# Layers' turned rows in 128-byte pieces, other PSUM banks, other prices for the listing

## The chip, the cores and the metric

The kernel runs on one core of a Trainium2 chip. The time is device microseconds of the whole execution on that core. The engines are TensorE (PE; its weight loads are listed apart as PEld), VectorE (DVE), ScalarE (ACT), GpSimd (POOL) and SyncE (SP), which here only issues transfers. Before the change three runs gave a median of 1317.81 us (1317.18 to 1320.26).

## What is computed

128 graphs of 64 nodes with 256 features each run through four layers, each with a layer normalisation ahead of it and a residual sum behind it. All numbers are float32.

```python
h = relu(layernorm(x)); x = x + L0(h, adj)   # attention, 4 heads: softmax over edges, then elu
h = relu(layernorm(x)); x = x + L1(h, adj)   # attention, 1 head
h = relu(layernorm(x)); x = x + L2(h, adj)   # gated relations; entries of adj are 0 or 1, so only relation 1 counts
h = relu(layernorm(x)); x = x + L3(h, adj)   # 3 steps: a = A^T (h W_i), then a GRU cell on (a, h)
```

In an attention layer the weight of edge (i, j) is exp(leaky_relu(s_i + d_j)) over its sum, where s and d are products of the node's row with two vectors. Up to a factor that the sum takes out, this is the larger of two products, so the kernel makes exp((alpha - 1) s_i), exp(d_j) and exp(alpha d_j) and combines them with max. For adjacencies with entries over 1 a general path exists, which isn't entered here.

## The kernel before

**Tiling.** Two graphs of 64 nodes fill the 128 partitions, and four such pairs make a group (`G = 4`, 512 rows). There are 16 groups. Each goes through layers 0, 1 and 2 (`attention` at line 1383, twice, and `loop_relation` at 1473) and then three steps of the recurrence (`Recurrence.step` at 1059). The products of the recurrence are most of the kernel's: a step has 42 products of 128 x 128 by 256 columns, each of two passes. Two groups' recurrences alternate, and the layers of later groups lie between them.

**The order of the work is written by a planner.** All instructions are recorded first (`Plan.note` at 254, called by `Engine` at 539; so almost all of them have line 549 in the profile, and those of `beside` have 841). Then `Plan.emit` (503) lists them with modelled durations (`cost` at 583): it runs forward and backward `PASSES` times with a random seed `SEED`, takes the best, shifts jobs by the numbers in `MOVES`, and emits the result. So each engine has a fixed order, and waits in it. For a transfer, `cost` takes bytes over a rate that hangs on the tile's tag. Where the listing sees PE idle in the first 115 us, it emits filler products (`nc.spare`, line 1638, `sz<-warm`), one for each 220 ns of that idle time (line 530).

**PSUM.** There are eight banks. `Banks.room` (1231) gives `sy` two, `sz` three, and three to a shared tag `mt`, which serves `tp`, `tq`, `mm` and `mn`. The recurrence's sets of seven products (`Sevens` at 1066) take one `sy` and one `sz` bank each; there are four sets in a step, 192 in all.

**The turned rows of the layers.** The products of layers 0 to 2 need the normalised rows with features on partitions. For the first two groups PE transposes them (`layernorm_T`, 695). For the other 14 groups `layernorm_T_by_dma` (734) does so, 42 times: ScalarE writes the normalised rows `hn`, VectorE turns blocks of 32 x 32 into `tb`, one transfer takes `tb` to DRAM (`way`, 512 KB), four more bring it back to `land`, each into 32 partitions (1 KB pieces), and two ScalarE copies of 512 columns put it in its place in `hT`. `tb` and `land` share the buffers `hn`, so the trace has them as `hn`. The recurrence has its own round trips through `way`, to `hnat` and `hT`, which also serve the start of a recurrence.

**Edges and exponentials.** Each group's adjacency is loaded thrice: `at` as four transfers of 32 KB (two graphs of a pair on the free axis), `ag` with 128 nodes on the partitions, and `eg` turned. `edge_bounds` (1365) makes from `at` a bound for each edge, transposed by PE. For the 14 later groups, `attention` brings the s exponentials `fs` onto all partitions: PE transposes `fs`, VectorE copies it to `fT`, one transfer writes `row` to DRAM, and two read it back to `t`, the same to all 64 partitions of a half.

**Queues.** Almost all transfers go through SP's queue, in its fixed order.

Of the kernel before, what the change touches and what calls it, by code (L numbers as in the profile page):

```python
# [10 lines left out]
F32 = mybir.dt.float32  # L11
# [6 lines left out]
S = 32  # L18
# [9 lines left out]
NEG1 = -9000000000000000.0  # L28
ALPHA = 0.2
EPS = 1e-5  # L30
BIG, TINY = 3.0e38, 1.0e-24
BOUND = 6.25
NREL = 39
RC = 5
# [188 lines left out]
class Plan:  # L223
# [30 lines left out]
    def note(self, engine, call, cost, writes, reads, after=(), port=0.0, dma=False):  # L254
# [23 lines left out]
            b.ops.append(op)  # L278
        return op

    PASSES, SEED, SPREAD = 27, 39, 50.0
    MOVES = (
        10, 12, 18, 24, 27, 28, 58, 71, 83, 84, 89, 99, 118, 129, 136, 141, 144, 198, 214, 221, 266, 299, 322, 324,
        334, 341, 346, 390, 400, 412, 424, 434, 550, 559, 579, 611, 616, 682, 785, 808, 825, 869, 910, 1123, 1323,
        1710, 1729, 1754, 1784, 1908, 1924, 1933, 2133, 2158, 2174, 2755, 2883, 3921, 3988, 4026, 4270, 4596, 4876,
        4885, 5049, 5501, 5547, 5750, 5954, 6055, 6156, 6434, 6590, 7283, 7340, 7414, 7540, 7602, 7657, 7774, 7857,
        7930, 7942, 8201, 8457, 8683, 8685, 9083, 9436, 9811, 9967, 10320, 10820, 10999, 11484, 11701, 12627, 12696,
        12718, 12783, 12858, 12980, 13024, 13178, 13347, 13474, 14022, 14057, 14422, 14846, 16253, 16751, 16786,
        17194, 18227, 19571, 21611, 22526, 22951, 22990, 23107, 24055, 25299,
    )  # L290
    LEEWAY = {"PE": 100.0, "DVE": 100.0, "Activation": 100.0, "Pool": 100.0, "SP": 300.0, "-": 0.0}
    OVERLAP = {"DVE": 83.0, "Activation": 95.0, "Pool": 43.0}
# [210 lines left out]
    def emit(self):  # L503

        self.on = False
        self.link()
        best, self.random = None, Random(self.SEED)
        for _ in range(self.PASSES):
            ranks = [op.due for op in self.ops]
            end, order = self.forward()  # L510
            if best is None or end < best[0]:
                best = end, ranks, [op.start for op in self.ops]
            self.backward(end)
        end, ranks, starts = best
        jobs = list({id(op.job): op.job for op in self.ops}.values())
        for j in jobs:
            j.sum, j.count, j.shift = 0.0, 0, dict.fromkeys(self.RANKED, 0.0)
        for op, start in zip(self.ops, starts):
            op.job.sum, op.job.count = op.job.sum + start, op.job.count + 1
        for m in self.MOVES:  # L520
            self.move(m, end, jobs)
        for op, due in zip(self.ops, ranks):
            op.due = due + op.job.shift.get(op.engine, 0.0)
        end, order = self.forward()
        best = end, [(op, op.start, op.idle, op.places) for op in order]
        self.ends = best[0]
        for op, start, idle, places in best[1]:
            op.start = start
            if op.engine == "PE" and self.spare and start < 115.0 * 1e3:
                for _ in range(int((idle - 100.0) / 220.0)):  # L530
                    self.spare()
            for b, tag in places:
                b.pool.make(b, tag)
            op.call()
        self.ops = []
        return best[0]
# [46 lines left out]
def cost(engine, method, args, kwargs):  # L583
# [4 lines left out]
        return (m / 1.2 + 2.5) * (1 if method == "transpose" else 2)  # L588
    if engine == "sync" or method == "dma_start":
        to, of = args[:2]  # L590
        rate = {"way": 450.0, "fine": 220.0}.get(to.base.tag, 150.0) if isinstance(to, View) else 150.0
        if isinstance(of, View) and of.base.tag in ("way", "fine"):
            rate = 170.0 if of.base.tag == "way" else 125.0
        return n * to.shape[0] * 4 / rate
# [15 lines left out]
def kernel(  # L610
# [33 lines left out]
    xr = x.rearrange("b n d -> (b n) d").rearrange("(t q) d -> q t d", q=P)  # L644
    ar = adj.rearrange("b n m -> (b n) m").rearrange("(t q) m -> q t m", q=P)

    tr = adj.rearrange("(t r a) i j -> t a i r j", r=2, a=2)
    er = adj.rearrange("(t r a) j i -> t r j a i", r=2, a=2)
    outr = out.rearrange("b n d -> (b n) d").rearrange("(t q) d -> q t d", q=P)

# [7 lines left out]

    same = nc.kept(const, [P, P], F32, name="same")
    diag = nc.kept(const, [P, N], F32, name="diag")  # L660
    amax = nc.kept(const, [P, NG], F32, name="amax")
    flag = nc.kept(const, [1, 1], I32, name="flag")
    wc = nc.kept(const, [P, LAYERS, K, 3 * D], F32, name="wc")
    whh = nc.kept(const, [P, K, 3 * D], F32, name="whh")
# [69 lines left out]
    def layernorm_T_by_dma(work, dram, src, hT, natural=None):  # L734
# [50 lines left out]
        nc.vector.transpose(  # L785
            tb.rearrange("p j k n c -> p n k j c"), hn.rearrange("p n (k j b) -> p n k j b", k=K, b=S)
        )
        way = dram.tile([P, P // S, K * n * S], F32, name="way")
        nc.sync.dma_start(way, tb.rearrange("p j k n c -> p j (k n c)"))
        land = work.tile([P, P // S, K * n, S], F32, name="land")  # L790
        for j in range(P // S):
            nc.sync.dma_start(
                land[j * S : (j + 1) * S].rearrange("p i x c -> p i (x c)"),
                way[:, j].rearrange("(i b) x -> b i x", b=S),
            )
        for a in range(2):
            nc.scalar.copy(
                hT[:, a].rearrange("p k n (e c) -> p (k n) e c", c=S),
                land[:, 2 * a : 2 * a + 2].rearrange("p e x c -> p x e c"),
            )  # L800

    def transpose_blocks(psum, dst, src, rblocks, scale=1.0, turned=False):
# [416 lines left out]
    with ExitStack() as s1:  # L1219
# [4 lines left out]
        class Banks(Pool):  # L1224
# [4 lines left out]
            early = psum = spare = True  # L1229

            def room(self, tag, base):
                return {"mt": 3, "sy": 2, "sz": 3}.get(tag, 1)


            def tile(self, shape, dtype, name, **kwargs):
# [31 lines left out]
        class Layer:  # L1267

            place = {"em": "hn", "dg": "hn", "tb": "hn", "land": "hn"}

            shared = {"hn": 3, "o": 2, "st": 4, "mv": 4, "var": 4, "rstd": 4, "nm": 4, "rec": 4, "fT": 1}

            def __init__(self, layer, pool, bufs):
                self.layer, self.pool, self.bufs = layer, pool, bufs
# [16 lines left out]
        for i, a in enumerate((a_src, a_dst)):  # L1293
            nc.scalar.dma_start(AB[:, i, :], over_partitions(a, D))
        nc.scalar.dma_start(w0e[:, :, :D], rows(W0))
        AT, XG, AG, EG = [], [], [], []

        def load_group(g):
            nc.begin(("load", g))
            xg = work.tile([P, G, D], F32, name="xg", bufs=5)  # L1300
            n = 2 if g == 0 else G
            for p in range(0, G, n):
                nc.sync.dma_start(xg[:, p : p + n], xr[:, g * G + p : g * G + p + n, :])
            at = work.tile([P, G // 2, 2, N], I32, name="at", bufs=3)
            for a in range(2):
                for u in range(G // 2):
                    edges = tr[g * G // 2 + u, a]
                    nc.sync.dma_start(at[a * N : (a + 1) * N, u], edges)
            AT.append(at)
            XG.append(xg)  # L1310

        def load_edges(g):
            ag = work.tile([P, G, N], I32, name="ag", bufs=4)
            nc.sync.dma_start(ag, ar[:, g * G : (g + 1) * G, :])
            AG.append(ag)
            eg = work.tile([P, G, N], I32, name="eg", bufs=2)
            for r in range(2):
                for u in range(G // 2):
                    nc.sync.dma_start(eg[r * N : (r + 1) * N, 2 * u : 2 * u + 2], er[g * G // 2 + u, r])
            EG.append(eg)  # L1320
# [44 lines left out]
        def edge_bounds(g):  # L1365


            at = AT[g]
            top = work.tile([P, G // 2, 2], F32, name="top")
            nc.vector.tensor_reduce(top, at, AX.X, ALU.max)  # L1370
            nc.vector.tensor_reduce(amax[:, g : g + 1], top, AX.XY, ALU.max)
            nc.vector.tensor_scalar(top, top, 0.0, TINY, op0=ALU.is_le, op1=ALU.mult)
            m = work.tile([P, G // 2, 2, N], F32, name="m", bufs=1)
            nc.vector.tensor_scalar(m, at, 0.0, BIG, op0=ALU.is_gt, op1=ALU.mult)
            nc.vector.tensor_tensor(m, m, top[:, :, :, None].to_broadcast([P, G // 2, 2, N]), ALU.max)
            pt = psum.tile([P, T], F32, name="tp")
            for u in range(G // 2):
                nc.tensor.transpose(pt[:, u * P : (u + 1) * P], m[:, u].rearrange("p g j -> p (g j)"), ident)
# [4 lines left out]
        def attention(g, p0, n, layer, heads, we, pool):  # L1383
# [31 lines left out]
                    )  # L1415
            else:

                fs = pool.tile([P, n, heads], F32, name="fs")
                nc.scalar.activation(fs, es[:, :, :heads], AF.Exp, scale=ALPHA - 1.0)
                pt = psum.tile([P, T], F32, name="tp")  # L1420
                nc.tensor.transpose(pt[:nh, :P], fs.rearrange("p g h -> p (g h)"), ident)
                fT = pool.tile([nh, P], F32, name="fT")
                nc.vector.tensor_copy(fT, pt[:nh, :P])
                row = dram.tile([2, nh * N], F32, name=f"row{layer}")
                nc.sync.dma_start(row.rearrange("a (c i) -> c a i", i=N), fT.rearrange("c (a i) -> c a i", i=N))
                for half in range(2):
                    nc.sync.dma_start(
                        t[half * N : (half + 1) * N].rearrange("p c i -> p (c i)"),
                        row[half : half + 1, :].to_broadcast([N, nh * N]),
                    )  # L1430
            flat = lambda d, c: d.rearrange("p g h -> p (g h)")[:, c, None].to_broadcast([P, len(range(nh)[c]), N])
            m = 2 if heads > 1 else n
# [95 lines left out]
        def before(g):  # L1528
            ABD[g] = work.tile([P, G, N], F32, name="abd")
            by_dma = dram if g >= AHEAD else None  # L1530
            START[g] = before_recurrence(W[3], psum, XG[g], AG[g], ABD[g], by_dma, g in PLAIN)

        def recur(g):
            return Recurrence(
# [99 lines left out]
        if 115.0:  # L1634
            warm = const.tile([P, P], F32, name="warm")
            nc.nc.vector.memset(warm, 1.0)
            pause = psum.real.tile([P, P], F32, name="sz", tag="sz", bufs=3)
            nc.spare = lambda: psum.spare and nc.nc.tensor.matmul(pause, warm, warm, start=True, stop=True)  # L1638
        with tc.manual_schedule(engines={getattr(mybir.EngineType, e) for e in ENGINES.values()}):
            nc.emit()  # L1640
# [215 lines left out]
```

## Time and profile before

One profiled execution took 1316.05 us, of which the span that the profile shows is 1314.2. TensorE had its full clock through it.

| What | Value |
|---|---|
| Median of the runs | 1317.81 us |
| The profiled execution, its span | 1316.05 us, 1314.2 us |
| Busy TensorE in the first 88 us | 85.04 us |
| Busy TensorE in the last 64 us | 54.77 us |
| DMA share of 16 engines: first 33 us, 88 to 1186 | 79%, 37% |
| Packets on SP's queue, their bytes | 132,072, 142.54 MB |
| Packets under 512 bytes | 43,417 of 132,782 |

Three rows of the trace about the pieces that the change touches: the filler, the transposes of the exponentials (two shapes, for layers 0 and 1), and the copies of them on VectorE. Columns are line, engine, operation, output and inputs, shape, count, then busy time in us, mean ns of one, and the idle time ahead of them.

```profile
L1638 PE MATMUL sz<-warm 128*128 128x128 f32 x168 | 24.5, 294 | 1.1 <-DVE mhalf L549 1.1
...
L549 PE MATMUL tp<-ident,fs 128*16 128x128 f32 x14 | 3.8, 273 | 0.0
L549 PE MATMUL tp<-ident,fs 128*4 128x128 f32 x14 | 3.8, 273 | 0.0
```

Products overlap in PE's pipeline, so the mean time of one (294 ns) is longer than the spacing of two (0.11 us in the timeline). A filler product is two passes, so 168 passes are 84 products.

The list of transfers has, with bytes of one and the median us from issue to landing:

```profile
way<-hn SPq DMA_DIRECT2D x42, 512.0 KB, 3.0
hn<-way SPq DMA_DIRECT2D x168, 128.0 KB, 3.1
```

The first is `tb` on its way to DRAM, the second the way back to `land`.

### The profile page before, as it was taken

The numbers are of one execution on the slowest core, as the hardware profiler recorded it, in microseconds if no ns is written. First come the engines' busy times: TensorE is split into PE (matmuls) and PEld (weight loads), VectorE is DVE, ScalarE is ACT, GpSimd is POOL, SyncE is SP. The second block draws the span as 40 slices with busy tenths as digits, with TensorE's granted clock in tenths as the row PEclk, the third lists the DMA queues.
The fourth block names the chain that finished last, engine by engine and source line by source line (L and its number), as shares of the span: only waits on it lengthen the run. The fifth ranks groups of instructions, "written<-read, shape, count | busy, mean of one in ns | idle before, by whom it ended". The sixth has DMA issues, their size and how long they took to land.

```text
span 1314.2 us, 27889 instructions
## 1 busy us (share of the span) xinstructions
PE 1298.9 (99%) x9837; PEld 1030.0 (78%) x9837; DVE 1058.3 (81%) x2562; ACT 856.6 (65%) x2173; POOL 694.3 (53%) x845
## 2 busy tenths in 40 slices
PE   9999999999999999999999999999999999999997
PEld 8667887878787777878778787877878788778885
DVE  6878667978879798897968889796887979786666
ACT  5867765666776676667766666776666667645543
POOL 2745744646555545546535564654556447445453
PEclk9999999999999999999999999999999999999999
DMA  7232122335334343443434344334334423142222
GB/s 229 66 101 58 53 85 89 110 121 161 110 117 143 115 138 94 144 122 116 126 118 142 92 150 120 104 122 132 113 104 143 132 86 129 38 129 65 65 65 68
DMA packets 132782, 144.94 MB, mean 110 GB/s; under 512 B 43417, under 2 KB 117913, under 8 KB 132633
## 3 DMA queue, kind: packets, MB, share of 16 engines
q1 hardware_dynamic: 132072, 142.54, 35.8%
q8 instruction: 80, 1.31, 0.4%
q10 hardware_dynamic: 560, 0.52, 0.1%
q14 instruction: 70, 0.57, 0.1%
HBM read 81.01 MB, written 61.49 MB: 108 GB/s over the span
## 4 chain that ended last, share of the span: by engine, by line
PE 85%; DVE 5%; ACT 5%; POOL 2%; issue 1%; DMA 1%; SPq 0%; ACTq 0%; DVEq 0%; POOLq 0%
PE sy L549 34%; PE sz L549 25%; PE mm L549 15%; PE mm L841 3%; PE tp L841 3%; ACT hn L549 2%; DVE hT L549 2%; PE sz L1638 1%; PE tp L549 1%; DVE t L549 1%; ACT hT L549 1%; PE tq L841 1%; DVE r L549 1%; POOL rstd L549 1%; DVE st L549 1%
## 5 line engine op out<-in xcount | busy, mean ns | idle before, releaser
L549 POOL TENSOR_TENSOR r<-hT,hT 128x256 f32<-128x256 f32 x192 | 156.2, 820 | 274.9 <-ACT hT L549 273.6
L549 DVE SCALAR_TENSOR_TENSOR hT<-r,hT 128x256 f32<-128x256 f32 (+1 forms) x290 | 182.4, 633 | 26.8 <-ACT r L549 24.5
L549 PE MATMUL sy<-hS,wsum 128*128 128x256 f32 x576 | 172.4, 383 | 1.2 <-ACT r L549 0.7
L549 PE MATMUL sy<-aS,wsum 128*128 128x256 f32 x576 | 172.4, 382 | 0.0
L549 PE MATMUL sz<-hS,whh 128*128 128x256 f32 x576 | 171.4, 383 | 0.6 <-DVE z L549 0.6
L549 PE MATMUL sz<-aS,wc 128*128 128x256 f32 x576 | 167.0, 383 | 0.8 <-DVE hT L549 0.8
L549 DVE TENSOR_TENSOR hT<-hT,sz 128x256 f32<-128x256 f32 x288 | 118.2, 410 | 39.5 <-PE sz L549 32.9
L549 ACT ACTIVATE hT<-hT,bi 128x256 f32<-128x256 f32 x192 | 95.7, 505 | 61.9 <-DVE hT L549 60.8
L549 POOL TENSOR_TENSOR aS<-aT 128x256 f32<-128x256 f32 x96 | 82.5, 859 | 94.0 <-ACT aT L549 94.0
L549 PEld LDWEIGHTS sy<-hS,wsum 128*128 128x128 f32 x576 | 106.8, 190 | 30.4 <-issue 9.4
L549 PEld LDWEIGHTS sy<-aS,wsum 128*128 128x128 f32 x576 | 107.6, 190 | 21.1 <-issue 4.2
L549 PEld LDWEIGHTS sz<-hS,whh 128*128 128x128 f32 x576 | 106.4, 190 | 22.4 <-issue 5.2
L549 PEld LDWEIGHTS sz<-aS,wc 128*128 128x128 f32 x576 | 106.9, 190 | 17.8 <-DVE hT L549 1.2
L549 ACT ACTIVATE hn<-xg,nm,rstd 128x256 f32<-128x256 f32 x200 | 108.0, 592 | 19.6 <-POOL nm L549 18.3
L549 ACT ACTIVATE hT<-sy,bh 128x256 f32<-128x256 f32 x192 | 90.2, 470 | 45.6 <-PE sy L549 42.4
L549 POOL TENSOR_TENSOR rstd<-var,mhalf 128x4 f32<-128x4 f32 (+1 forms) x70 | 78.1, 1115 | 77.0 <-ACT var L549 76.8
L549 PE MATMUL mm<-wl,hT 128*128 128x512 f32 x248 | 118.6, 594 | 0.0
L549 ACT COPY z<-sy 128x256 f32<-128x256 f32 x192 | 70.4, 367 | 64.9 <-PE sy L549 63.7
L549 DVE TENSOR_TENSOR hT<-hT,sy 128x256 f32<-128x256 f32 x192 | 79.3, 413 | 36.3 <-PE sy L549 34.1
L549 DVE BATCH_NORM_STATS2 st<-xg 128x6 f32<-128x256 f32 x256 | 96.3, 408 | 8.2 <-POOL xg L549 4.8
L549 DVE TENSOR_TENSOR z<-sz,z 128x256 f32<-128x256 f32 x192 | 79.5, 415 | 28.7 <-PE sz L549 27.2
L549 POOL TENSOR_TENSOR hS<-hT 128x256 f32<-128x256 f32 x96 | 80.0, 834 | 38.1 <-DMA hT<-way 15.2
(207 smaller groups left out, 3212.6 us busy)
## 6 DMA issues: line engine op xcount, KB each, us to landing
way<-tb SPq DMA_DIRECT2D x59, 512.0 KB, 2.7
hnat<-way SPq DMA_DIRECT2D x184, 128.0 KB, 3.0
way<-hn SPq DMA_DIRECT2D x42, 512.0 KB, 3.0
hn<-way SPq DMA_DIRECT2D x168, 128.0 KB, 3.1
xg<-in_x_dram SPq DMA_DIRECT2D x15, 512.0 KB, 4.4
out_dram<-xg SPq DMA_DIRECT2D x15, 512.0 KB, 2.9
t<-row SPq DMA_DIRECT2D x28, 256.0 KB, 4.1
hT<-way SPq DMA_DIRECT2D x52, 128.0 KB, 2.8
```

Of the source, the lines that this page charges most:

```text
L549: return do(*[real(a) for a in args], **{k: real(v) for k, v in kwargs.items()})
L841: nc.nc.tensor.matmul(*[real(x) for x in product], start=True, stop=True)
L1638: nc.spare = lambda: psum.spare and nc.nc.tensor.matmul(pause, warm, warm, start=True, stop=True)
```

## The change

- `layernorm_T_by_dma`, for layers 0 to 2: `tb` goes to DRAM in four transfers of 128 KB (`fine`), laid out so that two reads of 256 KB can put every 128-byte piece straight to its place in `hT`. `land` and the two ScalarE copies go.
- `attention`: VectorE's block transpose turns `fs` (padded to 32 columns; with one head GpSimd clears the rest), in place of a transpose by PE and a copy. Four transfers write `row` instead of one.
- One `at` of the shape of `ag` is loaded per group, in one transfer, and serves the bounds, too; `ag` goes. In `edge_bounds` the multiplication by `BIG` and the max become one instruction, with `BIG` at 1e29, and `amax` keeps a maximum for every row and pair.
- Banks: `sy` 2, `sz` 2, shared 4.
- The listing: other rates for transfers, 40 passes, another seed and other `MOVES`; filler in the first 12 us is one product for each 280 ns that the listing sees idle.

```diff
-    PASSES, SEED, SPREAD = 27, 39, 50.0
+    PASSES, SEED, SPREAD = 40, 28, 50.0
     MOVES = (
...
-                for _ in range(int((idle - 100.0) / 220.0)):
+                for _ in range(int((idle - 100.0) / (280.0 if start < 12e3 else 220.0))):
...
-        rate = {"way": 450.0, "fine": 220.0}.get(to.base.tag, 150.0) if isinstance(to, View) else 150.0
+        tag = to.base.tag if isinstance(to, View) else None
+        rate = {"way": 450.0, "fine": 220.0, "t0": 190.0, "t1": 190.0}.get(tag, 150.0 if tag in (None, "at", "eg", "o", "row0", "row1") else 290.0)
         if isinstance(of, View) and of.base.tag in ("way", "fine"):
             rate = 170.0 if of.base.tag == "way" else 125.0
...
-        way = dram.tile([P, P // S, K * n * S], F32, name="way")
-        nc.sync.dma_start(way, tb.rearrange("p j k n c -> p j (k n c)"))
-        land = work.tile([P, P // S, K * n, S], F32, name="land")
-        for j in range(P // S):
+        fine = dram.tile([2, P // S, S, 2, K * n * S], F32, name="fine")
+        for i in range(P // S):
             nc.sync.dma_start(
-                land[j * S : (j + 1) * S].rearrange("p i x c -> p i (x c)"),
-                way[:, j].rearrange("(i b) x -> b i x", b=S),
+                fine[i % 2, :, :, i // 2].rearrange("j b x -> b j x"),
+                tb[i * S : (i + 1) * S].rearrange("p j k n c -> p j (k n c)"),
             )
-        for a in range(2):
-            nc.scalar.copy(
-                hT[:, a].rearrange("p k n (e c) -> p (k n) e c", c=S),
-                land[:, 2 * a : 2 * a + 2].rearrange("p e x c -> p x e c"),
+        for e in range(2):
+            nc.sync.dma_start(
+                hT.rearrange("p a k n (e c) -> p (a k n) e c", c=S)[:, :, e],
+                fine[e].rearrange("j b a (x c) -> (j b) (a x) c", c=S),
             )
...
-                return {"mt": 3, "sy": 2, "sz": 3}.get(tag, 1)
+                return {"mt": 4, "sy": 2, "sz": 2}.get(tag, 1)
...
-            m = work.tile([P, G // 2, 2, N], F32, name="m", bufs=1)
-            nc.vector.tensor_scalar(m, at, 0.0, BIG, op0=ALU.is_gt, op1=ALU.mult)
-            nc.vector.tensor_tensor(m, m, top[:, :, :, None].to_broadcast([P, G // 2, 2, N]), ALU.max)
+            m = work.tile([P, G // 2, 2, N], F32, name="m", bufs=1)
+            nc.vector.scalar_tensor_tensor(
+                m.rearrange("p u r j -> p (u r) j"), AT[g], BIG,
+                top.rearrange("p u r -> p (u r)")[:, :, None].to_broadcast([P, G, N]), op0=ALU.mult, op1=ALU.max,
+            )
...
-                fs = pool.tile([P, n, heads], F32, name="fs")
-                nc.scalar.activation(fs, es[:, :, :heads], AF.Exp, scale=ALPHA - 1.0)
-                pt = psum.tile([P, T], F32, name="tp")
-                nc.tensor.transpose(pt[:nh, :P], fs.rearrange("p g h -> p (g h)"), ident)
-                fT = pool.tile([nh, P], F32, name="fT")
-                nc.vector.tensor_copy(fT, pt[:nh, :P])
+                fs = pool.tile([P, S], F32, name="fs")
+                used = 2 * nh
+                if used < S:
+                    nc.gpsimd.memset(fs[:, used:], 0.0)
+                nc.scalar.activation(fs[:, :used], es.rearrange("p g h -> p (g h)"), AF.Exp, scale=ALPHA - 1.0)
+                fT = pool.tile([P, S], F32, name="fT")
+                nc.vector.transpose(fT, fs)
```

## The prediction

> **What bounds the kernel now.** I read the busy shares first, then the stretches, then the opening of the timeline, and last the rows that the change touches.
>
> ```profile
> PE 1298.9 (99%) x9837; PEld 1030.0 (78%) x9837; DVE 1058.3 (81%) x2562; ACT 856.6 (65%) x2173; POOL 694.3 (53%) x845
> ...
> PE 85%; DVE 5%; ACT 5%; POOL 2%; issue 1%; DMA 1%; SPq 0%; ACTq 0%; DVEq 0%; POOLq 0%
> ```
>
> ```profile
> 88.00:1186.00 1098.00, 1096.54 (x8416) 866.22 (x8415) 910.66 (x2185) 732.33 (x1836) 589.26 (x691) 1.00 0.37 112
> ```
>
> The first line gives busy time per engine, the second the chain of waits by engine, the third one stretch (its length, then the busy time of PE, weight loads, VectorE, ScalarE and GpSimd, then granted clock, DMA share and GB/s). In the 1098 us in the middle TensorE is idle for 1.5 us, at full clock. A busy PE need not be at its peak, so I check its pace: the chain has eight passes of `sy` in 1.73 us, again and again, which is 0.216 us for each 256 columns, without a break. So in the middle, time goes only if PE work goes, and it comes back only if PE is made to wait. VectorE (81%) and ScalarE (65%) have room.
>
> At the start it is different:
>
> ```profile
> 1.06 11.23 PE L1638 MATMUL sz<-warm 128*128 128x128 f32 x80 [1.06 <-DVE mhalf L549]
> ...
> 6.88 1.09 ACT L549 ACTIVATE hn<-xg,nm,rstd 128x256 f32<-128x256 f32 x2 [1.11 <-POOL nm L549]
> ...
> 12.13 0.60 PE L549 MATMUL tp<-ident,hn 128*128 128x128 f32 x4
> ...
> 12.57 2.62 PE L1638 MATMUL sz<-warm 128*128 128x128 f32 x22
> 12.77 0.66 ACT L549 ACTIVATE hT<-tp 128x256 f32<-128x256 f32 x2 [4.51 <-PE tp L549]
> ```
>
> (Timeline: start, duration, engine, line, operation.) The `sz<-warm` products are filler: the listing puts one in for each stretch that it believes PE idle. The first normalised rows `hn` are ready at 6.88 + 1.09 = 7.97, but the transposes that want them start at 12.13, because 80 filler passes stand ahead of them. Filler is the bottleneck there.
>
> **The change, part by part.** The instruction lists of the two built programs say how many of each kind there are; the durations are of the trace of before.
>
> *Filler: 84 products become 40* (40, 11, then 33 scattered; now 28, 3, then 9). Each is two passes.
> - First block: 80 passes took 12.13 - 1.06 = 11.07 us, 0.138 each. 56 take 7.7 and end at 8.8. The new ScalarE order puts the second half's small rows ahead of `hn`, so that `hn` is ready at about 8.8 too. Gain 3.3 us.
> - Second block: 22 passes, 0.112 apart, become 6. Gain 1.8. ScalarE now writes all four `hn` together, not two of them after the relu that waited 4.51 us, so the next rows are there.
> - The other 66 become 18: 48 × 0.112 = 5.4 us at most. In the timeline the next real work mostly follows its filler at once, so it was ready by then, but not how long before. I count two thirds, 3.6.
>
> *The 28 `fs` transposes leave PE.* Their twins, four `tp<-ident,hn` from 12.13 to 12.57, are 0.11 us apart: 28 × 0.11 = 3.1 us, all of it in the stretch where PE is never idle. VectorE gets 28 block transposes of 32 columns in place of 28 copies of 0.27 us; its rows of 512 columns (0.693 us) and 1024 (1.240) give a line that has about 0.18 at 32. All that VectorE does for them gets shorter (28 × 0.09 = 2.5 us), as do the bounds (16 × (0.366 + 0.145) = 8.2 us gone, from `m<-at` and `amax<-top`): nothing on PE, the end is not VectorE's.
>
> *The turned rows.* Seen once in each of 42 layer normalisations.
>
> ```profile
> L549 ACT COPY hT<-hn 128x512 f32<-128x512 f32 x84 | 49.0, 615 | 5.2 <-DMA hn<-way 5.0
> ```
>
> These 84 copies go, 49 us of ScalarE, off the path. What stays to be paid is the latency. Before, by the list of DMA issues: one `way` write (3.0 us), four reads issued 0.43 apart that land in 3.1 (4.4 in all), two copies of 0.61: 8.6 us. Now: four writes of 128 KB issued 0.43 apart, the last landing at 1.3 + 3.0 = 4.3; then two reads of 256 KB, each 2048 pieces of 128 bytes. The nearest row is the last group's `hT<-tb`, also in 128-byte pieces, alone on the queue:
>
> ```profile
> DMA packets 4077, 0.49 MB, mean 49 GB/s; under 512 B 4077, under 2 KB 4077, under 8 KB 4077
> ...
> q1 hardware_dynamic: 4077, 0.49, 32.2%
> ```
>
> That is a window of 10 us: 0.322 × 16 × 10 / 4077 = 12.6 ns a piece. 4096 pieces on 16 engines are 3.2 us, plus the 1.9 us or so that the small ones (2.0 to land, 0.2 of it moving) spend otherwise: 5.1. Sum 9.4 us, 0.8 later than before. The listing's own price of the two reads is 2 × 262,144 / 125 = 4.2 us, so it expects them 1.0 us later than this row does, and places the consumers accordingly. I take nothing lost. **A rule speaks against it:** the Trainium skill's page *DMA: Bandwidth & Descriptors* (Specifications) asks for at least 512 bytes for line rate, below which a piece costs a read-modify-write. If a 128-byte piece costs what nearly 512-byte ones do (the final stores: 562 packets, 0.27 MB, 16.4% of 5.5 us, 25.7 ns), the reads take 6.6 us, 2.4 more than planned; over 42 turns up to 101 us. By the row it is none. I follow the row, which is of this size, but it reads SBUF where the new reads come from DRAM, so the other end stays open.
>
> In sum over the span the pieces add 42 × (4096 × 12.6 - 512 × 57) / 16 = 59 us of the 16 engines (57 ns is queue 1's mean packet, 35.8% of 16 × 1314.2 over 132,072): their share goes from 36 to about 40%. Not a bound.
>
> *SP's queue* gets 62 more transfers net (168 `fine` writes, 84 reads, 112 `row` writes in; 210 `way`/`hn`, 28 `row`, 64 net of `at`/`ag` out). At 0.45 us each 28 us over 1314: no bound. But SP waits in order. Each transfer also waits for one some eight places ahead in the list, so the six parts of a turn fill the slots, and `hnat<-way` and `hT<-way` of the recurrences stand behind a read that waits for its writes for 4.3 us instead of 3.0. GpSimd waited 15.2 us for `hT<-way` and POOL is 53% busy, so this has cover. At the start it helps: 8 small `at` loads of the first two groups become 2 and no longer hold slots, and the weights `hhn` go from eighteenth to eleventh.
>
> *`row`:* four writes where there was one adds 3 × 0.43 = 1.3 us, and the trip through PE's queue is gone; even.
>
> *Banks:* `sz` 3 to 2, shared 3 to 4. PE waited 1.4 us in all for releases ahead of `sz`; `sy` always had two and waited 2.6 in all. Between a loss of some 2 us and a like gain for `tp`, `mm`: zero.
>
> *Order.* The new list has the first `sy` after 14 us less PE work than before (9.6 of it filler), so the recurrences start earlier; the tail of pure recurrences is the same work.
>
> **Sum:** 3.3 + 1.8 + 3.6 + 3.1 = 11.8 us. From the profiled execution, 1316.05 (span 1314.2 and 1.9 around it), that is 1304.2; the median of the runs is 1.8 above that, so **1306 us**.
>
> **Rivals.**
> - *Half is given back (1312).* The scattered fillers stood where PE would have waited anyway, and the second block too, for loads: DMA is 79% busy in the first 33 us. Then only 3.3 + 3.1 remain. For it: PE already waits a little at the start. Against: loads leave earlier.
> - *The 128-byte reads are late (1346).* PE now reads `hT` straight from the landing. With 42 turns, 11.8 us are eaten from 0.28 us mean lateness on, and 0.37 makes it slower: the piece price at which this holds is (4.2 + 0.37) × 16 / 4096 = 17.9 ns. At 20 ns, between the two prices above, they are 0.95 late: 42 × 0.95 = 40, 1306 + 40. For it: the source is DRAM. Against: 12.6 ns measured.
> - *The new order doesn't hold (1325).* It was made from other transfer prices and two `sz` banks; 0.1 us more at each of the 192 sets of products would take 19 us: 1306 + 19. From 0.08 us each it is slower. For it: the other two changed together. Against: the waits ahead of `sz` in the middle are next to none now.
>
> **How the numbers follow.** Forecast 0.68 (1299 to 1311), half given back 0.15, late reads 0.09, order 0.08. A run can tell 0.3% (4 us) from nothing: faster is below 1313.9. The forecast and most of the first rival lie there, 0.68 + 0.12; same 0.08, the rest of it with milder forms of the other two; slower 0.12. The low end, 1296, has all of the filler (1.8 more) and some 8 us of better order; the high end, 1317, takes in the first rival and the start of the other two.
>
> **What will show it.** Right: first `tp<-ident,hn` at 8.8 to 9.3 us; `sz<-warm` x80; no `fs` on PE, PE busy near 1287; PE idle in the middle still about 0.1%; DMA share 40%; last `hT<-fine` read landing about 4 us. Wrong: `mm` rows that wait for DMA `hT<-fine` by more than 10 us together (the second rival), or PE idle ahead of `sz` for VectorE (the third).

## The result, and the profile after

The changed kernel takes **1314.09 us** (median of 9 runs, 1312.59 to 1316.81) against 1317.34 for the kernel before beside it: a ratio of 0.9975, 95% interval 0.9966 to 0.9984. It is faster by 3.3 us, where 11.8 were forecast.

The page of the changed kernel: busy time per engine, the share and packets of SP's transfers (queue 1), the chain of waits by engine, and three rows of the transfers with their size and median us to landing. Its profiled run took 1316.71 us, near the upper end of its nine, with a span of 1314.9.

```profile
PE 1286.3 (98%) x9721; PEld 1022.2 (78%) x9721; DVE 1049.2 (80%) x2530; ACT 814.8 (62%) x2089; POOL 696.5 (53%) x859
...
q1 hardware_dynamic: 305472, 140.77, 44.4%
...
PE 75%; DVE 9%; POOL 5%; ACT 3%; DMA 3%; issue 3%; SPq 1%; DVEq 0%; POOLq 0%; ACTq 0%
...
fine<-hn SPq DMA_DIRECT2D x168, 128.0 KB, 2.3
hT<-fine SPq DMA_DIRECT2D x84, 256.0 KB, 4.3
...
t<-row SPq DMA_DIRECT2D x28, 256.0 KB, 4.0
```

TensorE's work fell as forecast (1286.3 busy, 1287 expected), but the chain that was 85% PE is 75% PE now, and VectorE, GpSimd and DMA have taken the rest. The same stretch as before, by engine:

```profile
88.00:1186.00 1098.00, 1086.18 (x8275) 864.39 (x8277) 895.34 (x2137) 690.43 (x1744) 590.37 (x699) 1.00 0.47 112
```

PE is idle for 11.8 us of these 1098, where it was idle for 1.5. That is where most of the gain went. Over the whole span PE's busy time fell by 12.6 us and its idle time rose by 13.4: 2.0 ahead of the first `sy` product, 10.3 from there to 1186 us, 1.1 behind that. The first `sy` runs at 94.1 us instead of 105.9, but not all of these 11.8 us are gained: 9.3 are filler, some 4.4 are work that the new order puts behind it, and 2.0 are lost again as idle time. From there to the end the span is 1220.8 us, where it was 1208.3.

What ended PE's waits between 88 and 1186 us (total us, times, longest), in the changed kernel:

```profile
PE mm L843 <- issue: 3.5, 3, 2.1
PE sy L553 <- ACT r L553: 3.1, 3, 1.8
PE sz L553 <- DVE hT L553: 2.1, 4, 0.7
```

and in the kernel before:

```profile
PE sy L549 <- ACT r L549: 0.7, 2, 0.5
PE sy L549 <- ACT z L549: 0.2, 1, 0.2
PE mm L841 <- DVE t L549: 0.2, 1, 0.2
```

So several kinds of wait are new, and no one of them is most of it. The largest gap ends at 448 us. The timeline of the changed kernel (start, duration, engine, line, operation, and in brackets the idle time ahead of it with what ended it):

```profile
435.80 0.22 ACT L553 ACTIVATE fs<-es 128x8 f32<-128x8 f32 x1
...
436.66 2.11 SPq L553 DMA_DIRECT2D row<-fT  x4
...
439.10 1.31 DVE L553 STREAM_TRANSPOSE tb<-hnat 128x512 f32<-128x512 f32 x2 [1.06 <-DMA way<-tb]
...
440.43 0.34 SPq L553 DMA_DIRECT2D way<-tb  x1
...
440.88 1.28 SPq L553 DMA_DIRECT2D t<-row  x2
...
446.57 0.42 DVE L553 TENSOR_TENSOR t<-t,gd 128x256 f32<-128x256 f32 x1 [5.45 <-DMA t<-row]
...
448.22 0.40 PE L843 MATMUL mm<-wh,t 64*64 64x257 f32 x1 [2.07 <-issue]
```

Read it downward. The exponentials are there at 436.0 and turned at 436.6. The four `row` writes hold SP until 438.8, and the last has landed at 439.8. The reads leave only 1.1 us after that, since a recurrence's `way<-tb` stands ahead of them in SP's order and waits for VectorE's `tb` (439.10 + 1.31). The second read lands at 446.5, 4.9 us after its issue, and VectorE, which has stood for 5.45 us, gets its `t`. PE's products that want the finished `t` start 2.07 us late. The view calls that "issue", but the row above shows who was late. Elsewhere it is mostly the `row` write that holds the reads: SP waits for one ahead of them 24 times. Over the stretch from 88 to 1186, PE's gaps ahead of `mm<-wh,t` add up to 4.2 us; before it was 0.2.

The waits for a DMA in the changed kernel (total us, times, longest):

```profile
POOL hS L553 <- DMA hT<-way: 25.8, 7, 7.0
POOL xg L553 <- DMA hnat<-way: 24.1, 9, 5.9
DVE t L553 <- DMA t<-row: 20.0, 14, 5.4
```

Before, these three were 15.2, 10.7 and 1.4 in total. PE itself never waits for `hT<-fine`.

The second largest gap (1.76 us, ended at 395.7) has another cause. One GpSimd power, which takes 1.06 us in the median, took 4.38; the normalised rows waited for it, ScalarE's queue behind them, and so did PE. The same three engines in the timeline:

```profile
388.53 4.38 POOL L553 TENSOR_TENSOR rstd<-var,mhalf 128x4 f32<-128x4 f32 x1 [2.80 <-ACT var L553]
...
393.23 2.07 ACT L553 ACTIVATE hn<-xg,nm,rstd 128x256 f32<-128x256 f32 x4 [3.61 <-POOL nm L553]
...
395.71 0.81 PE L553 MATMUL sy<-hT,whh 128*128 128x256 f32 x2 [1.76 <-ACT r L553]
```

The gap cost more than its own length. The stretches around it (length, PE busy, granted clock, DMA share, GB/s):

```profile
392.80:396.20 3.40, 1.64 (x14) 1.00 1.02 195
396.20:399.60 3.40, 3.36 (x8) 0.50 0.23 35
```

Right behind it PE had half its clock for 3.41 us, with passes of 256 columns 0.427 us apart instead of 0.216; by these two an estimated 1.7 us more, counted as busy. The runs that follow differ in this, so a single trace is no exact balance: two profiled runs of the same kernel (both edits, below) are 4.2 us apart.

At the start, filler still stands ahead of the first transposes, and for longer than forecast:

```profile
1.06 9.36 PE L1641 MATMUL sz<-warm 128*128 128x128 f32 x56 [1.06 <-DVE warm L1639]
...
8.60 2.22 ACT L553 ACTIVATE hn<-xg,nm,rstd 128x256 f32<-128x256 f32 x4
...
10.26 0.60 PE L553 MATMUL tp<-ident,hn 128*128 128x128 f32 x4
10.70 0.83 PE L1641 MATMUL sz<-warm 128*128 128x128 f32 x6
11.37 0.60 PE L553 MATMUL tp<-ident,hn 128*128 128x128 f32 x4
```

56 passes took 9.20 us, 0.164 each, where I had counted 0.138. Start to start in the records, the first 27 are 0.213 apart, until 7.0 us; after that it is 0.111. Before, that pace of 0.213 ended at 5.3 us, so PE did not have its full clock from the first product on. The 24 passes that the change took out of this block were those 0.111 apart, 2.7 us; the slow pace lasted 1.7 us longer here, which cost 0.8 of them.

### The profile page after: what moved, and what is told of

The parts are those of the page before. It is cut to its first block, busy times and chain, and to the rows that moved or that the text cites. A ratio compares the mean times of both kernels' runs of the same rounds, so it can differ in the third digit from the quotient of the medians.

```text
span 1314.9 us, 27495 instructions
## 1 busy us (share of the span) xinstructions
PE 1286.3 (98%) x9721; PEld 1022.2 (78%) x9721; DVE 1049.2 (80%) x2530; ACT 814.8 (62%) x2089; POOL 696.5 (53%) x859
## 3 DMA queue, kind: packets, MB, share of 16 engines
q1 hardware_dynamic: 305472, 140.77, 44.4%
## 4 chain that ended last, share of the span: by engine, by line
PE 75%; DVE 9%; POOL 5%; ACT 3%; DMA 3%; issue 3%; SPq 1%; DVEq 0%; POOLq 0%; ACTq 0%
PE sy L553 31%; PE sz L553 23%; PE mm L553 14%; PE mm L843 3%; PE tp L843 3%; DVE hT L553 2%; DVE t L553 2%; ACT hn L553 2%; DMA t<-row 1%; SPq L553 1%; POOL r L553 1%; DVE st L553 1%; POOL rstd L553 1%; DVE hn L553 1%; PE sz L1641 1%
## 5 line engine op out<-in xcount | busy, mean ns | idle before, releaser
L553 POOL TENSOR_TENSOR aS<-aT 128x256 f32<-128x256 f32 x96 | 79.4, 828 | 95.6 <-ACT aT L553 95.6
L553 POOL TENSOR_TENSOR rstd<-var,mhalf 128x4 f32<-128x4 f32 (+1 forms) x70 | 83.9, 1198 | 75.4 <-ACT var L553 70.5
L553 POOL TENSOR_TENSOR xg<-xg,hn 128x1024 f32<-128x1024 f32 (+1 forms) x32 | 72.9, 2278 | 60.2 <-DVE hn L553 60.2
```

The costliest lines, as they stand in the source:

```text
L553: return do(*[real(a) for a in args], **{k: real(v) for k, v in kwargs.items()})
```

## The experiments

Theory: 128-byte pieces hold up SP's queue, so that what stands behind them lands late. Rivals: the rows of `t` alone, the filler, the new order. A transfer's issue on SP takes 0.3 to 0.6 us; the trace of before has 17 issues over 1 us, that of the changed kernel 72 (22 of `hnat<-way`, 14 of `fine<-hn`, 12 of `hT<-fine`). The rows of the two `fine` transfers on SP's queue in the changed kernel (issue time in ns, least, median and longest):

```profile
L553 SPq DMA_DIRECT2D fine<-hn x168: 302/435/3052, 36.1 to 1143.6; - x168
L553 SPq DMA_DIRECT2D hT<-fine x84: 517/547/4259, 41.6 to 1146.8; - x84
```

The medians are ordinary. It is some transfers that take several times that, and everything behind them in the queue with them. The Trainium skill's page *Perfetto Trace Analysis* (DMA Instruction — HWDGE) says that this time runs from the satisfied semaphores until the descriptors are made and the sequencer is free again, and that more descriptors can be made than their buffer holds. The times agree with that; no run here shows the buffer.

**Pieces of 1 KB.** The same bytes, in the same place of the order:

```diff
-hT.rearrange("p a k n (e c) -> p (a k n) e c", c=S)[:, :, e], fine[e].rearrange("j b a (x c) -> (j b) (a x) c", c=S)
+hT[:, :, e].rearrange("p a n j -> p a (n j)"), fine[e].rearrange("j b a x -> (j b) a x")
```

> The changed kernel, every engine's order kept word for word, but each of the 84 reads of hT from fine puts its 256 KB down in pieces of 1 KB and not of 128 bytes (so the values in hT are permuted, and layers 0 to 2 of the later 14 groups work on other numbers). Theory A (the 128-byte pieces hold up SP's queue and the engines, so that everything behind them lands late): issues over 1 us on SP's queue fall from 72 to about 20, the DMA share from 44 to about 37%, and the ratio to before falls from 0.9975 to 0.991 to 0.993 (1305 to 1309 us). Theory B (the longer trip of the exponentials, row and t, holds VectorE): VectorE's 20 us of waits for t stay above 12, ratio 0.996 to 0.998. Theory C (the listing's order itself, two sz banks): no change, 0.997 to 0.998.

Measured: 1312.58 us, 0.9957 (0.9944 to 0.9970) of before. Issues over 1 us fall from 72 to 23 and the DMA share from 44.4 to 37.0%. So the long issues come of the 128-byte pieces; this is shown. What they cost is less than theory A asked for (0.991 to 0.993): the ratio is 0.18% below the changed kernel's, with intervals that overlap. VectorE's wait for the rows stays at 16.9 us, 14 times, and GpSimd's two waits at 26.2 (`hnat<-way`) and 24.8 us (`hT<-way`). So the long issues are not what makes these two longer than before.

**No wait for the rows.** `t` is read from a weight in DRAM instead of `row`, so it waits for no write:

```diff
-row[half : half + 1, :n, 0].to_broadcast([N, n, heads * N])
+bass.AP(tensor=w_ih.tensor, offset=w_ih.offset, ap=[[0, N], [2 * heads * N, n], [1, heads * N]])
```

> The changed kernel in the same order, but t is filled from a weight in DRAM in the same pieces, so that its two transfers no longer wait for the four row writes (the attention weights of the later 14 groups are then not the reference's). Theory B (row trip): VectorE's wait for t falls from 20 us to under 4 and the ratio to 0.992 to 0.994. Theory A (128-byte pieces): the wait for t falls too, but the late landings of hnat, hT and the issues over 1 us stay, ratio 0.996 to 0.997. Theory C: no change, 0.997 to 0.998.

Measured: 1313.12 us, 0.9963 (0.9952 to 0.9973). The wait at `t` falls only to 14.6 us, in 7 places, where theory B had it under 4, and 73 long issues stay.

**Both edits.**

> The changed kernel in its own order with both edits of the first two experiments: hT in 1 KB pieces and t filled from a weight without waiting for row (numbers of the later 14 groups are then not the reference's). If late transfers are what took the forecast's missing 8 us: the two gains add or more than add, ratio 0.991 to 0.9935, VectorE's wait for t under 8 us. If the order itself has too little slack for any lateness (theory C): the gains overlap, ratio 0.995 to 0.9965, and TensorE is still idle 8 us or more between 88 and 1186 us.

Measured: 1307.89 us, **0.9928** (0.9915 to 0.9941). Repeated later beside other kernels:

> The kernel with 1 KB pieces and without the wait for the rows, a second time, beside the two that are to be compared with it. Both theories: 0.991 to 0.994 of the kernel before, SP issues over 1 us about 23.

1307.00 us, **0.9922** (0.9908 to 0.9936), 24 long issues. Against the changed kernel's 0.9975 the two edits together bring 0.47 to 0.53%, six to seven us. That is more than 0.18 + 0.12, though the intervals leave room for a plain sum. The two `fine` rows of the repeat:

```profile
L553 SPq DMA_DIRECT2D fine<-hn x168: 302/436/1342, 36.2 to 1136.1; - x168
L803 SPq DMA_DIRECT2D hT<-fine x84: 523/551/758, 41.7 to 1138.7; - x84
```

The medians are the same and the long ends are gone. PE's gaps ahead of `mm<-wh,t` are 1.3 us (4.2 in the changed kernel). So that these two parts of the change cost 6 to 7 us is shown by the times of both runs. How they cost them is shown only in part. VectorE still waits for `t` (13.8 us, in the repeat 11.9, where under 8 was expected), and PE is idle for 11.5 and 10.1 us between 88 and 1186, which was the sign of theory C. Between the profiled runs of the changed kernel and of the repeat, 6.9 us apart, the first `sy` is 1.8 us earlier, PE's idle time behind it 2.9 less and its busy time 2.4 less, of which the half clock is 1.7 by the estimate above.

**The read from ScalarE's queue.** `nc.nc.scalar.dma_start` in place of `nc.nc.sync.dma_start` for `hT<-fine`.

> The changed kernel in the same order, but the 84 reads of hT from fine are issued from ScalarE's own queue at the places where the listing has them, and no longer from SP's. All values are the reference's. Theory A in the form that SP's queue is held up while descriptors are made: issues over 1 us on SP fall to about 30, ratio 0.992 to 0.995 in spite of 84 x 0.55 us more on ScalarE. Theory A in the form that the 16 engines are busy with small pieces: landings stay late, ratio 0.997 to 0.999. Theory C: 0.998 to 1.000, since ScalarE only gets more to do.

Measured: 1321.10 us, 1.0024 (1.0015 to 1.0034). SP is free again (25 long issues), and the reads are long in ScalarE's queue instead: 17 of the 84 take over 1 us there, up to 3.7. So the hold goes with the queue that issues the small pieces. But ScalarE, in its own fixed order, now waits for `fine<-hn` to land, too, and PE's idle time in the middle grows from 11.8 to 17.1 us. The ratio fits none of the three forms.

**Twice the bytes in each write.** On the kernel with both edits, `fine` doubled in DRAM:

```diff
-tb[i * S : (i + 1) * S].rearrange("p j k n c -> p j (k n c)")
+bass.AP(tensor=w.tensor, offset=w.offset, ap=[list(w.ap[0]), [96, 8], [1, 256]])   # 8 pieces of 1 KB, not 4
```

> The kernel with 1 KB pieces and without the wait for the rows, but each write to fine carries twice its bytes in 1 KB pieces (512 more pieces a layer's group of graphs, some 30 us more of DMA engine time; the 128-byte reads carried 1536 pieces and 15 us more than the 1 KB reads; the hidden rows' values are moved within the layer's turned rows). Theory that SP is held by the engines' busy time: as many long issues as with the 128-byte pieces or more (70 to 110), and the 1.5 us or more that the large pieces had brought are lost (0.994 to 0.998 of the kernel before). Rival, that SP is held by the count of pieces: 30 to 45 long issues, and 0.992 to 0.995.

Measured: 1321.33 us, 1.0032 (1.0023 to 1.0041), 14.3 us above the repeat of both edits. 76 long issues, which is the number for busy engines. But 36 of them are the doubled writes themselves:

```profile
L802 SPq DMA_DIRECT2D fine<-hn x168: 302/599/1927, 36.3 to 1149.2; - x168
L810 SPq DMA_DIRECT2D hT<-fine x84: 523/553/1655, 41.9 to 1153.3; - x84
```

Here the median of the writes grew, too, from 436 to 599. PE itself waits 6.0 us for `hnat<-way` there (0.3 in the changed kernel). Of the other transfers 40 are long, against 22 with both edits and 58 in the changed kernel. To set these side by side the sizes have to be put right: the expectation counted the pieces and the engine time of one 128-byte read, and a turn has two. Per turn the 128-byte pieces add 3584 pieces and 30 us of the engines over large ones, the doubled writes 512 pieces and 31 us (60.8 ns each). With a seventh of the pieces and the same engine time, SP is held again, though its other transfers are long less often than in the changed kernel. So busy engines suffice to hold SP, which speaks against the count of pieces as the whole cause; that the count has a part isn't excluded. The time is no clean measure here, since the `fine` transfers also land 0.9 us later (median 3.9, 3.0 with both edits), which by itself delays `hT`.

**The filler alone**, in the kernel before: `int((idle - 100.0) / (280.0 if start < 12e3 else 220.0))`.

> The kernel before with one edit alone: filler in the first 12 us is one product for each 280 ns of idle time and not 220. If the filler overran at the start, as the prediction has it: first transposes at about 9.5 us instead of 12.1 and a ratio of 0.9975 to 0.9985 (2 to 3.3 us). If the loads set the start: first transposes earlier, but the ratio 0.9995 to 1.0005, because the next wait is for a load.

Measured: 1316.99 us, 0.9993 (0.9984 to 1.0001). 9 products fewer, and no difference that can be told. The first transposes came at 10.6 us instead of 12.1 and the first `sy` 1.5 us earlier, but PE's idle time in the middle was 3.4 us instead of 1.5. The other way round, on the kernel with both edits, the old rule (`/ 220.0` throughout):

> The kernel with 1 KB pieces and without the wait for the rows, with filler in the first 12 us by the rule of the kernel before (one product for 220 ns of idle time: 9 products, 18 passes more). Theory that filler past the doubling of PE's pace is paid in full once nothing else is late: 18 passes of 0.111 us, so 1.0 to 2.0 us more than the run beside it with the new rule (0.9985 to 0.9992 as new against old). Rival, that the saving is lost later anyway, as in the run that changed the filler alone: within 0.6 us.

Measured: 1310.05 us, 0.9954 (0.9938 to 0.9971), so in that kernel the new rule is worth 0.32% by the ratios, 3.05 us by the medians of 5 and 6 runs; the first `sy` moves by 1.9 us (94.2 to 92.3). The expectation of 1 to 2 us lies within what the two intervals allow. It goes the way of the first theory: cut filler counts once other things are not late. With so wide an interval, and profiled runs that don't differ (1309.52 with the old rule, 1309.79 with the new), I call it likely, not shown.

**The changed and the old order without their lists.** `MOVES = ()` in each.

> The changed kernel with an empty MOVES, so that its order comes from the passes alone. Theory C (the tuned order is tight, and slips when it meets real latencies): against the same listing's times this order slips less than the changed kernel's 21 us over the span, about 10, so it is slower than the changed kernel by less than its listing says; ratio to before 1.000 to 1.006. If the parts of the change (pieces, row trip, two banks) cost the time whatever the order: the slip stays near 20 us and the ratio is 1.008 or more.

> The kernel before with an empty MOVES, the partner of the run without MOVES of the changed kernel. The ratio of the two is the change without either's hand-picked shifts. Parts that pay by themselves (14 us less work on TensorE): the changed one is faster by 0.5% or more. Parts that cost what they save: within 0.3% of one another. Own expectation: before without MOVES 1.006 to 1.012 of before.

Measured: 1328.24 us, 1.0083 (1.0070 to 1.0096), and 1325.11 us, 1.0057 (1.0044 to 1.0070). Without their lists the changed kernel is thus slower by 1.0083 / 1.0057, 0.26%, though its first `sy` is 15.1 us earlier (94.1, 109.3): PE's idle time in the middle is 15.0 us, where it is 6.0. By the expectation this is the case in which the parts cost time whatever the order. The list chosen for the changed kernel is worth 1.1%, that for the kernel before 0.6%. So the change gains only together with its list; each of the two is one order of many.

**Three kernels with another list of moves.** All three compute the reference's values, with a list chosen for other modelled durations. The first takes the turned rows as before, the second keeps the 128-byte pieces, the third is the first with less filler. From the first one's edit:

```diff
-    MOVES = (4, 9, 12, 15,
...
+    MOVES = (94649, 142652, 70317,
...
-"t0": 190.0, "t1": 190.0
+"t0": 150.0, "t1": 150.0
```

> The changed kernel with the layers' turned rows taken as before (one transfer to way, four back in large pieces, two ScalarE copies), all else of the change kept (rows of t by DMA, exponentials turned by VectorE, banks, filler), durations in the listing set nearer to the changed kernel's trace (rows of t 150 bytes/ns, normalisation 400 + 0.73 n, power of eight columns 1250 ns) and the list of moves chosen anew for it (106 moves). Correct values. Theory that the 128-byte pieces hold SP's queue: SP issues over 1 us back near 25, dynamic-queue DMA share 36 to 38 %, VectorE's wait for the rows of t under 17 us, and 0.990 to 0.995 of the kernel before. Rival, that what is missing comes of the rows of t alone: SP issues may fall but the time stays at 0.996 to 0.999.

Measured: 1318.54 us, 1.0003 (0.9994 to 1.0013). SP has 26 long issues and a share of 35.6%, as expected, but the time isn't: GpSimd now waits 63.1 us for `hnat<-way` (24.1 in the changed kernel). That the new list puts the recurrences' own transfers too close is my reading of it, not shown. The rows and the list changed at once, and the run can't tell them apart.

> The changed kernel with its 128-byte pieces kept, the listing's durations set nearer to its trace as in the run beside it, and the moves chosen anew (60 moves). Correct values. Theory that the 128-byte pieces hold SP's queue: no list of moves can give it back, SP issues over 1 us stay near 70, 0.996 to 0.999 of the kernel before, over 0.3 % above the run with old rows. Rival, that the list of moves did not fit the durations: as low as the run with old rows, 0.990 to 0.995.

Measured: 1316.10 us, 0.9985 (0.9979 to 0.9992), 65 long issues. No better than the list it replaced, nor the 0.3% worse than the run with old rows that was expected. Of the kernels that compute the reference's values, the changed one with 1314.09 us remains the fastest.

> The run with old rows, and filler in the first 12 us given one product for every 400 ns of idle time instead of 280. Correct values. Theory that filler passes cost 213 ns each until PE's pace doubles, some 6 us after its start, whatever their number: 5 to 10 products fewer save 0.5 to 2 us against the run with old rows (0.9985 to 0.9996 of it). Rival, that fewer products delay the doubling and the first transposes pay for it: no saving, or 1 us lost.

Measured: 1319.86 us, 1.0015 (1.0008 to 1.0023), 1.3 us above the run with old rows. The rival holds, and the trace shows why. The windows of this run (length, PE busy, granted clock, DMA share, GB/s):

```profile
10.00:12.00 2.00, 0.29 (x3) 0.77 1.05 335
12.00:14.00 2.00, 1.81 (x7) 0.50 0.98 273
14.00:16.00 2.00, 2.00 (x7) 0.50 1.02 336
16.00:20.00 4.00, 4.00 (x18) 0.76 1.07 346
```

The first transposes did come earlier (7.5 us, 8.8 in the run with old rows). But with ten products gone PE stood idle from 7.8 to 9.1 us and for most of 10 to 12, its granted clock fell to 0.50, and it was not back at 1.00 until the window from 20 us. The first `sy` came 3.6 us later (96.1, 92.5). Not every run lost its clock: of the 18, the five with a mean granted clock of 0.998 took 1318.5 us on average, as the run with old rows does, and the six with 0.995 or less took 1321.5. The Trainium skill's page *TensorE: Matmul & The Clock Gate* (Part 1) has this: a clock halved after an idle window of some 3.4 us and full again after a busy one. Here an interval with PE mostly idle sufficed, two idle stretches with a few passes between them. So filler is a price for the clock, and below some number it is worth paying.

## Why the prediction was wrong

**The direction was right, the size was not.** The step that failed is that the sum takes nothing off for what happens behind the start: the turned rows' "I take nothing lost", SP's "no bound" and "*`row`*: even", and with them the supposition that PE's idle time in the middle stays at 0.1%. It was 11.8 us of 1098, 1.1%. The turned rows' pieces and the wait for `row` together cost 6 to 7 us of the 8.5 that are missing, as the two edits show; the order, and the two `sz` banks in it, has a part, too.

*Filler.* From the start of each block of passes to the next product, in the records of both traces:

| Term | Forecast | Measured |
|---|---|---|
| First block | 3.3 us | 11.07 - 9.20 = 1.9 |
| Second block | 1.8 | 2.46 - 0.67 = 1.8 |
| Scattered | 3.6 | 8.23 - 2.58 = 5.6 |
| All filler | 8.7 | 9.3 |

The sum held by luck of two errors. The first block was priced at a mean pace of 0.138 us, though the pace has two values, and the passes that go are of the shorter one. Of the scattered filler it counted two thirds, and all of it went. But the table is filler time, not time saved: ahead of the first `sy` PE is idle for 5.0 us, where it was 3.0.

*The 28 transposes of `fs`* left PE; their 3.1 us are within the fall of PE's busy time (1298.9 to 1286.3).

*The turned rows.* By their own price they went as forecast: landing in 4.3 us, a 128-byte piece 14.9 ns in the packet records (12.6 estimated, 17.9 the point from which the rival with late reads decided, 25.7 by the prediction's reading of the rule in the Trainium skill's *DMA: Bandwidth & Descriptors*, Specifications, which no run here bears out), and no `mm` waiting for `hT<-fine`. What I asked was when the pieces land, not how long they hold SP's queue: 72 long issues for 17. I had counted SP's time as 62 more issues at their mean of 0.45, 28 us. All issues together grew from 380 to 475 us. By itself the change to 1 KB pieces brought 1.5 us, within the noise; together with the other edit it counts for more.

*`row`.* Four writes hold SP for 2.26 us on average, where one held it for 0.29. That is 2.0 more, not 3 × 0.43 = 1.3. The way through PE's queue that is gone saved 1.5 (from the start of `fs` to the first write, 2.51 then and 1.00 now). So `t` is asked for 0.3 us later on average (4.07 us after the start of `fs` then, 4.41 now). That is nearly even. But the listing expects a read of `t` to land 2.89 us after its issue, with its new rate of 190 bytes/ns, and it takes 3.55; before, it expected 3.24 and 3.33 were measured. The order is built for a `t` that comes sooner: 14 waits, 20 us of VectorE, 4.2 us of PE.

*DMA share:* 44.4%, not 40. I took all old pieces away at queue 1's mean and gave nothing to the writes, which go in 1 KB pieces now (60.8 ns each on the mean) where `way` went in 4 KB ones (178 ns): 42 × (512 × 60.8 - 128 × 178) / 16 = 22 us. The pieces at 14.9 instead of 12.6 are 25 us more. Over 16 engines' span that is 3.5 points.

*Banks.* They were counted as zero, and the third rival's sign was PE idle ahead of `sz` for VectorE. In the middle that is 2.1 us now, in four gaps where PE waits until VectorE has read an `sz` bank, and none before. The rival thus came true in a small part. *VectorE* was right at nothing: its work fell by 9 us without effect.

*Order.* The forecast took it that the new order feeds PE as well as the old one did. The listing that the changed kernel's own code makes says otherwise: in its modelled times PE is idle for 5.9 us between 88 and 1186, where the listing of the kernel before has 1.6 (measured: 11.8 and 1.5). Its gaps stand at products where the traces have them, 0.37 ahead of `sz<-hS,whh` at 206 (0.74 at 210 in the changed kernel) and 0.73 ahead of `sy<-aT,wc` at 1169 (1.13 at 1181 in the repeat of both edits). So idle time of half the measured size was in the plan already. The two listings end 11.3 us apart all the same, since that of the changed kernel has the first `sy` at 90.4 us; in the trace it is at 94.1.

*What stays open.* Both edits recover 6 to 7 us of the 8.5 missing, and the kernel with them (0.9922, about 10 us gained) comes near the forecast. But it isn't the forecast's own account: its trace still has 10.1 us of idle PE in the middle, made good by a first `sy` that is earlier still (92.3). One gap, 0.70 us at 541 to 546, stands in all eight traces of the new order, so it doesn't come of the transfers that the edits change. I didn't trace each. The two `sz` banks, the single `at` and the new rates weren't tested alone. Nor is it settled what part the count of pieces has beside the engines' busy time in holding SP.

## What to carry to other kernels

A transfer in small pieces has two prices, its own landing and the time it holds its queue; for the second, list the issues that take several times their median, and not only the mean. Where a middle stretch has no idle time, taking work out of it brings only as much as the other engines and transfers have slack: count how late each of the next ones may be before adding the savings up, and read the idle time that the new plan itself has. Before removing filler, look at its pace in the trace, block by block, and at what the clock does without it.

## What the hardware showed unexpectedly

- The pace of the opening passes, 0.213 us, ended between 4.0 and 7.2 us after the span's start in 15 traces, and at 5.4 to 7.2 among kernels with nearly the same opening. The row of the granted clock reads 1.00 during all of it, but that is no reading: in each trace the record of the clock begins only where the pace doubles (5.36 us before, 7.05 in the changed kernel), and a window without a record prints 1.00. The Trainium skill's page *TensorE: Matmul & The Clock Gate* (Part 1) puts the change some 4 us into the work, half a us either way. Here the first product is at 1.06 us and the spread is wider.
- About half a window of idle time was enough to halve the clock. Cut into windows of 3.41 us from the start of each trace's clock record, PE at full clock was idle for 1.94 us or more in 17 windows, and the clock was halved behind every one; at 1.72 or less it never was. Between these, at 1.75 to 1.89, four were followed by half clock and four were not. The same gap of 1.76 us near 395 thus halved the clock in two kernels (the changed one, the read from ScalarE's queue) and not in the repeat of both edits.
- One GpSimd power, at 386 to 389 us, took 4.38 us in four traces (the changed kernel, the read from ScalarE's queue, both edits twice), and in four others with the same order of the work there no power took over 1.76. Each time PE then stood for 1.75 or 1.76 us. What sets it off isn't known.
- The same VectorE operation (`abd<-ag` before, `abd<-at` after) took 0.28 us before (0.275 to 0.295) and 0.26 to 2.43, 0.92 on average, in the changed kernel. All that took over 0.4 us stood beside GpSimd work there, but before the change six that did so for most of their time took 0.28 to 0.29. It wasn't tested alone.
